# Reordering the start of a two-layer transformer kernel: the DMA queue's order and the first tile's place on TensorE

## The chip, the core and the metric

The kernel runs on one core of a Trainium2 chip. The core has a matrix engine (TensorE, PE in the profile), a vector engine (VectorE, DVE), an activation engine (ScalarE, ACT), a general engine (GpSimd, POOL) and a sync engine (SyncE, SP) that here only issues DMAs. Each engine works through its own instructions in order and waits on semaphores where it needs another's result. SP, ACT and POOL can issue DMAs, and the profile counts 16 DMA engines that carry them.

The metric is the device time of one execution in microseconds (us). The kernel before was timed three times: 1159.06, 1164.08 and 1165.76 us, so its median is 1164.08 us. The execution that the profiler recorded took 1164.43 us.

## The reference, cut to what matters

Two layers work on `x` of shape (2, 1024, 256). Each layer normalises `x` and adds an attention and a feed-forward result to it. The change is in layer 0's attention, at its very beginning:

```python
xn = _layernorm(x)
q = (xn @ Wq + bq).reshape(B, T, 32, 8).transpose(0, 2, 1, 3)     # 32 heads of 8
k = (xn @ Wk + bk).reshape(B, T, 8, 8).transpose(0, 2, 1, 3)      # 8 K/V heads
v = (xn @ Wv + bv).reshape(B, T, 8, 8).transpose(0, 2, 1, 3)
q = q * cos + rotate_half(q) * sin
k = k * cos + rotate_half(k) * sin
scores = einsum('bhqd,bhkd->bhqk', q, repeat(k, 4)) / sqrt(8)
scores = where(kpos > qpos, -inf, scores)
out = einsum('bhqk,bhkd->bhqd', softmax(scores), repeat(v, 4)) @ Wo + bo
x = x + out + ffn(xn)                                             # then layer 1, of the same kind
```

## The kernel before

**Tiles and chunks.** The 2048 rows of `x` are 16 tiles of 128 (`xs[0]` to `xs[15]`) and 4 chunks of 512. Layer 0's attention (`attention0`) goes over query tiles `(b, i)`: batch 0 from `i = 0` to 7, then batch 1 from 7 down to 0. Tile `(0, 0)` is called the first tile here, `(0, 1)` the second, and so on. A chunk's Q and K are made by `project` (L829 the matmuls, L840 the multiplication with the rope table on DVE), written to DRAM in three bf16 parts and read back in another layout.

**Two passes over a tile.** A softmax needs each row's maximum. So each tile has a pass of `max_unit`s (L992 the products, L964 the mask, L1004 the reduction on DVE), one for each pair of heads or for a few of them; then `take_max` (L1012) splits the 32 maxima of each row into three parts, `turn_max` (L1025) turns them on PE, copies them on ACT (`mts`, L1029), writes them to DRAM (`mscr`, L1031) and reads them back as three more rows of the Q tile (`qlast<-mscr`, L1033). With these rows the second product subtracts the maximum by itself. This second pass is `weigh` (L1056): the tile's scores `s`, their exponential `p` on ACT (L1066), the causal triangle on POOL (L1070), and `gather` (L1086), which adds up `p` times V in PSUM.

**The order on PE is written out.** In `attention0` the order of PE's instructions is the order in which Python emits them. `one_slot` (L1281) is the clock: each slot lets `advance` emit some `max_unit`s, in an order and at a rate worked out beforehand, with one step from `extra` (layer norm, projections of chunk 1, and so on) after a unit; then `tick` runs what `after(slots, f)` had put off. The main loop (L1301) does `weigh` for a tile, one pair of heads and K block per slot, but first runs slots without `weigh` until the tile's `take_max` lies `LEAD` slots back, or `SHORT` slots for the first three tiles. `wait_busy` (L1269) puts matmuls without use in front of a unit: 55 in front of unit 0, and 10 in front of unit 5, the first one of the second tile.

**The DMA queue.** Nearly all transfers of this stretch are issued by SP, in one order. In the first chunk, `prepare_q` (L881) sends the first tile's part of Q to DRAM from ACT and keeps the three other tiles' parts, two writes each, in `unsent`. `load_q` (L906) then reads a tile back with eight transfers: per half, two of 24 rows by 4 KB, one of 16 rows and one of 8 rows. The loop at L1156 emits for tiles 1, 2 and 3 the two writes and then the eight loads, with chunk 1 of `x` (four tiles) after tile 1. Then follow `bo`, the rope table of chunk 1 (`load_rope(1)`), `wo` and the eight tiles of `x` of batch 1. `issue_after(ins)` only orders an instruction behind `ins` on its engine. SP's transfers share eight semaphores in turn, and one whose semaphore is still in use by the eighth transfer before it waits for that one.

Of the kernel before, what the change touches and what calls it, by code (L numbers as in the profile page):

```python
# [37 lines left out]
TAIL = 16  # L38
LEAD = 10
SHORT = 6  # L40
LN_EPS = 1e-5
RMS_EPS = 2.0**-23
E4_MIN = 2.0**-6
# [5 lines left out]
def two_layers(ctx: ExitStack, tc: tile.TileContext, a: dict, out: bass.AP):  # L49
# [9 lines left out]
    def load_x(lo, hi):  # L59
        for i in range(lo, hi):  # L60
            nc.sync.dma_start(out=xs[i], in_=x_flat[i * P : (i + 1) * P, :])
# [43 lines left out]
    def load_rope(c):  # L105
        nc.sync.dma_start(out=rope[:, :, c * 512 : (c + 1) * 512], in_=a["rope0"][:, :, c * 512 : (c + 1) * 512])
# [7 lines left out]
    def load_weights(pool, names):  # L114
        w = []
        for name in names:
            n = a[name].shape[1]
            t = pool.tile([P, 2, n], F32, tag=name, name=name)
            nc.sync.dma_start(out=t, in_=a[name].rearrange("(k p) n -> p k n", p=P))
            w.append(t)  # L120
        return w
# [17 lines left out]
    def keep_busy(out, n):  # L139


        rhs = ident_bf[:, None, :].to_broadcast([P, 4, P])
        for _ in range(n):
            nc.tensor.matmul(out.rearrange("p (h q) -> p h q", h=4), groups, rhs, start=True, stop=True)  # L144
# [14 lines left out]
    def behind():  # L159
        return tc.issue_after(mark[0].ins)  # L160

    def rsqrt(pool, src, n, eps, name):

        v = pool.tile([P, n], F32, tag="rs_v", name=f"rs_v{name}", bufs=1)
        s = pool.tile([P, n], F32, tag="rs_s", name=f"rs_s{name}", bufs=1)
        y = pool.tile([P, n], F32, tag="rs_y", name=f"rs_y{name}", bufs=2)
        nc.vector.tensor_scalar(v, src, eps, None, ALU.add)
        nc.scalar.activation(s, v, AF.Sqrt)
        nc.vector.reciprocal(y, s)
        nc.vector.tensor_mul(s, y, y)  # L170
        nc.vector.tensor_mul(s, s, v)
        nc.vector.tensor_scalar(s, s, -0.5, 1.5, ALU.mult, ALU.add)
        nc.vector.tensor_mul(y, y, s)
        return y

    def layernorm(L, chunks, lp, pp, tag):
# [4 lines left out]
        for i in range(n):  # L181
# [3 lines left out]
            if i % 4 == 3:  # L185
                yield
        rs = rsqrt(lp, mv[:, :n, 1], n, LN_EPS, f"ln{nm}")
        yield
# [583 lines left out]
    def attention0(w, qlast, tables):  # L772
# [11 lines left out]
        with ExitStack() as es:  # L784
# [8 lines left out]
            last_load = [None]  # L793
# [112 lines left out]
            def load_q(b, i):  # L906

                qst[b, i] = [
                    pool.tile([P, NH0 // 2, P], BF, tag="qmain", name=f"qmain_{b}{i}", bufs=len(qlast)),
                    qlast[len(qst) % len(qlast)],  # L910
                ]
                for e in range(2):
                    parts = scratch[b, i, e].rearrange("a (d h) t -> a d (h t)", d=HD0)
                    for n, row, lo, hi in ((0, 0, 0, 3), (0, 24, 0, 3), (0, 48, 0, 2), (1, 0, 2, 3)):
                        row += HALF * e
                        last_load[0] = nc.sync.dma_start(
                            out=qst[b, i][n][row : row + HD0 * (hi - lo)].rearrange("p h t -> p (h t)"),
                            in_=parts[lo:hi],
                        )
# [5 lines left out]
            def prepare_v(b, c):  # L925
                v = vst[b]
                for kt in range(4 * c, 4 * c + 4):
                    ps = ps_t.tile([P, KV0, HD0], F32, tag="t", name=f"vp0_{b}_{kt}")
                    for k in range(2):
                        nc.tensor.matmul(  # L930
                            ps.rearrange("p g d -> p (g d)"),
                            xnT[2 * b + kt // 4][:, k, (kt % 4) * P : (kt % 4 + 1) * P],
                            wv[:, k, :],
                            start=(k == 0),
                            stop=(k == 1),
                        )
                    nc.vector.tensor_tensor(
                        v[:, kt, :, 0:HD0], ps, bv_bc.rearrange("p (g d) -> p g d", d=HD0), ALU.add
                    )


            slot = 0
            later = []

            def after(slots, f):
                later.append((slot + slots, f))
# [25 lines left out]
            def wait_busy(n):  # L972
                if n:
                    keep_busy(ps_t.tile([P, 512], F32, tag="t", name=f"busy{slot}_{n}"), n)
# [37 lines left out]
            def take_max(b, i):  # L1012
                both = mx.pop((b, i))
                m = both[:, 0].rearrange("p e n -> p (e n)")
                parts = pool.tile([P, 3, NH0], BF, tag="mparts", name=f"mp{b}{i}", bufs=1)
                r = pool.tile([P, NH0], F32, tag="mrest", name=f"mr{b}{i}")
                if i > 3:
                    nc.vector.tensor_tensor(both[:, 0], both[:, 0], both[:, 1], ALU.min)
                nc.vector.tensor_copy(parts[:, 0], m)
                nc.vector.tensor_tensor(r, m, parts[:, 0], ALU.subtract)  # L1020
                nc.vector.tensor_copy(parts[:, 1], r)
                nc.vector.tensor_tensor(parts[:, 2], r, parts[:, 1], ALU.subtract)
                after(3, lambda: turn_max(b, i, parts))

            def turn_max(b, i, parts):  # L1025
                ps = ps_t.tile([P, P], BF, tag="t", name=f"mt{b}{i}")
                nc.tensor.transpose(ps[: 3 * NH0], parts.rearrange("p a h -> p (a h)"), ident_bf)
                mt = pool.tile([3 * NH0, P], BF, tag="mt", name=f"mts{b}{i}", bufs=2)
                nc.scalar.copy(mt, ps[: 3 * NH0])  # L1029
                scr = dram.tile([3 * NH0, P], BF, tag="mscr", name=f"mscr{b}{i}")  # L1030
                nc.sync.dma_start(out=scr, in_=mt)  # L1031
                for e in range(2):
                    nc.sync.dma_start(  # L1033
                        out=qst[b, i][1][HALF * e + AUG : HALF * e + AUG + 3],
                        in_=scr.rearrange("(a e n) t -> e a n t", a=3, e=2)[e],
                    )
# [116 lines left out]
                prepare_q(0, 0, e)  # L1153
            load_q(0, 0)

            for i in range(1, 4):  # L1156
                with tc.issue_after(last_load[0].ins):
                    for j, send in unsent:
                        if j == i:
                            last_load[0] = send(nc.sync, i)  # L1160
                with tc.issue_after(last_load[0].ins):
                    load_q(0, i)
                if i == 1:
                    with tc.issue_after(last_load[0].ins):
                        load_x(4, 8)
            with tc.issue_after(last_load[0].ins):
                nc.sync.dma_start(out=bo_bc, in_=a["bo"][None, :].to_broadcast([P, D]))
            with behind():
                prepare_v(0, 0)
                for _ in range(3):  # L1170
                    next(conversions)
            with tc.issue_after(last_load[0].ins):
                load_rope(1)
                (wo,) = load_weights(zp, ("wo0",))
            with tc.issue_after(last_load[0].ins):
                load_x(8, NT)
# [80 lines left out]
            at = 0  # L1257
# [4 lines left out]
            done_at = {}  # L1262

            def advance():
                nonlocal at, credit, cost_left
                n, cost, unit = maxima[at]
                ready.extend(extra.pop(n, ()))

                wait_busy({0: 55, 4 + 1: 10}.get(at, 0))  # L1269
                unit()  # L1270
                if ready:
                    ready.pop(0)()
                at += 1
                credit -= cost
                cost_left -= cost
                if cost == 0:
                    done_at[n] = slot
                    if n >= 3:
                        next_weights()
# [21 lines left out]
            for n, (b, i) in enumerate(order):  # L1301
                if n and n + 3 < len(order):
                    load_q(*order[n + 3])
                while n not in done_at or slot < done_at[n] + (LEAD if n > 2 else SHORT):
                    one_slot(False)
                for G in range(2):
                    for j in range(i + 1):
                        for u in range(2):
                            one_slot(True)
                            if u and waiting:  # L1310
                                gather(*waiting)
                            group += weigh(b, i, 2 * G + u, j)
                        waiting = (b, i, G, j, group)
                        group = []
# [109 lines left out]
```

## Time and profile before

| What | us |
|---|---|
| three runs | 1159.06, 1164.08, 1165.76 |
| the profiled execution | 1164.43 |
| its span, first to last instruction | 1162.7 |
| PE busy | 1007.4 (87%) |
| DVE busy | 788.7 (68%) |
| ACT busy | 589.0 (51%) |
| POOL busy | 407.1 (35%) |
| first max unit of the first tile on PE | 42.64 |
| first product of the second tile on PE | 56.90 |
| first `weigh` of the first tile | 92.95 |

The span is what the trace covers; the device time of the same execution is 1.7 us more. A busy share is an average over both layers. What the change is worth is read from the first 140 us, where layer 0's attention starts. In the timeline each row gives the start, the duration, the engine, the line, the operation with what it writes and reads, how many of them are merged in the row, and in brackets how long the engine was idle before it and what ended that. `SPq` rows are DMA issues: they show when SP issued a transfer, not when it landed. Landings come from the trace's semaphore events.

### The profile page before, as it was taken

The page shows a single profiled execution, that of the slowest core. Times are in us where ns is not written, and L with a number is a line of the kernel's source. Part 1 is how long each engine was busy: PE and PEld are TensorE (multiplying, and loading weights), DVE is VectorE, ACT ScalarE, POOL GpSimd, SP SyncE. Part 2 cuts the span into 40 slices and gives each one's busy share as a digit, 9 for nine tenths or more (in the row PEclk, how much of TensorE's full clock was granted, in tenths as well). Part 3 has the DMA queues.
Part 4 walks back from the last instruction along what each step waited for, and adds up shares of the span by engine and source line. Part 5 has one row for each costly group of instructions (what it writes and reads, how often), then busy time and mean ns, then how long its engine had stood idle before and what let it go on. Part 6 is the DMA issues. An engine that isn't in the chain of part 4 may idle for free. (4 is left out here: it accounts for less than half of the span.)

```text
span 1162.7 us, 19973 instructions
## 1 busy us (share of the span) xinstructions
PE 1007.4 (87%) x7671; PEld 483.5 (42%) x7707; DVE 788.7 (68%) x1476; ACT 589.0 (51%) x1061; POOL 407.1 (35%) x440
## 2 busy tenths in 40 slices
PE   5858786887988989897989999885999999999798
PEld 3333331232432312232223333323567667667576
DVE  7467988899697998789896988605453554444421
ACT  2004461674456757576876777754354443443431
POOL 2007223424136121412134244547444535433400
PEclk9758896998899989998999999998899999989889
DMA  5432101101102010100000100007611432341200
GB/s 177 118 109 70 48 2 39 21 21 42 53 2 55 1 28 10 29 18 7 22 8 21 27 13 19 5 1 92 92 38 39 74 77 51 59 88 34 39 20 20
DMA packets 65928, 49.05 MB, mean 42 GB/s; under 512 B 20904, under 2 KB 59432, under 8 KB 65832
## 3 DMA queue, kind: packets, MB, share of 16 engines
q1 hardware_dynamic: 60632, 39.05, 15.0%
q0 software_dynamic: 4112, 8.26, 3.0%
q8 instruction: 60, 0.98, 0.4%
q10 hardware_dynamic: 1088, 0.46, 0.1%
q14 instruction: 36, 0.29, 0.1%
HBM read 34.12 MB, written 15.20 MB: 42 GB/s over the span
## 5 line engine op out<-in xcount | busy, mean ns | idle before, releaser
L1004 DVE TENSOR_REDUCE mx<-m 128x1 f32<-128x512 f32 (+3 forms) x608 | 372.4, 653 | 91.9 <-PE m L992 53.7
L1066 ACT ACTIVATE p<-s 128x512 f32<-128x512 f32 x576 | 307.1, 606 | 132.1 <-PE s L1056 129.6
L1086 PE MATMUL acc<-p,v 128*9 128x512 f32 x1152 | 170.8, 612 | 2.4 <-ACT p L1066 1.2
L1070 POOL TENSOR_SCALAR_AFFINE_SELECT p<-p 128x512 f32<-128x512 f32 x128 | 84.3, 681 | 157.7 <-ACT p L1066 157.4
L992 PE MATMUL m<-k,qmain 64*128 64x512 bf16 (+3 forms) x384 | 94.3, 356 | 49.7 <-DVE mx L1004 39.2
L992 PE MATMUL m<-kmain,qmain 64*128 64x512 bf16 (+3 forms) x384 | 83.1, 333 | 24.8 <-DVE mx L1004 22.7
L992 PEld LDWEIGHTS <-qmain 64*128 64x128 bf16 x768 | 50.1, 99 | 79.8 <-issue 50.9
L964 PEld LDWEIGHTS <-ident_h 64*128 64x128 bf16 x832 | 45.4, 97 | 88.0 <-issue 65.1
L964 PE MATMUL m<-mask_q,ident_h 64*128 64x128 bf16 (+3 forms) x832 | 75.0, 221 | 2.4 <-DVE mx L1004 2.2
L1056 PE MATMUL s<-qmain,k 64*128 64x512 bf16 x288 | 67.9, 395 | 9.0 <-ACT ob L275 3.1
L673 POOL TENSOR_TENSOR sq<-h 128x512 f32<-128x512 f32 x28 | 29.1, 1039 | 118.1 <-DVE h L669 118.1
L1056 PE MATMUL s<-qmain,kmain 64*128 64x512 bf16 x288 | 64.3, 390 | 5.3 <-ACT p L1066 2.6
L1056 PE MATMUL s<-qlast,k 35*128 35x512 bf16 x288 | 63.9, 390 | 0.0
L514 DVE TENSOR_REDUCE m<-sq 128x16 f32<-128x2048 f32 x16 | 36.7, 2291 | 37.9 <-PE sq L506 36.3
L1056 PEld LDWEIGHTS <-k 64*128 64x128 bf16 (+1 forms) x576 | 21.1, 95 | 97.7 <-issue 89.6
L1056 PE MATMUL s<-qlast,klast 35*128 35x512 bf16 x288 | 61.3, 387 | 0.0
L659 PEld LDWEIGHTS <-wgu_bf 128*128 128x128 bf16 x384 | 38.4, 101 | 42.0 <-issue 5.8
L1129 POOL TENSOR_TENSOR x<-x,aos 128x256 f32<-128x256 f32 x16 | 12.0, 747 | 116.0 <-ACT aos L1128 116.0
L668 DVE SCALAR_TENSOR_TENSOR h<-h,f1gu 128x512 f32<-128x512 f32 x32 | 22.0, 686 | 41.7 <-ACT h L667 41.7
L697 PE MATMUL f1o<-k,hp 128*128 128x256 bf16 x384 | 46.1, 279 | 1.0 <-ACT vts L532 0.7
L541 PE MATMUL sk<-qs,ks 25*128 25x128 f32 x512 | 43.8, 423 | 3.1 <-DMA qs<-mscr 3.1
L457 PE MATMUL pqk<-k,xnT 128*128 128x512 f32 x64 | 37.5, 717 | 9.7 <-ACT all L478 9.3
(289 smaller groups left out, 1800.3 us busy)
## 6 DMA issues: line engine op xcount, KB each, us to landing
qmain<-qscr SPq DMA_DIRECT2D x64, 96.0 KB
qkv<-all SPq DMA_DIRECT2D x16, 384.0 KB
qscr<-ptq POOLq DMA_DIRECT2D x6, 384.0 KB, 4.2
x<-in_x SPq DMA_DIRECT2D x16, 128.0 KB
qmain<-qscr SPq DMA_DIRECT2D x32, 64.0 KB
qs<-qkv SPq DMA_DIRECT2D x16, 128.0 KB
ks<-qkv SPq DMA_DIRECT2D x16, 128.0 KB
vs<-qkv SPq DMA_DIRECT2D x16, 128.0 KB
```

Source lines behind the costliest of these rows:

```text
L457: nc.tensor.matmul(pqk, x[k], wqk[:, k, :], start=(k == 0), stop=(k == 1))
L514: nc.vector.tensor_reduce(m, ps, AX.X, ALU.max, negate=True)
L541: nc.tensor.matmul(ps[:, s, r, :], columns(k, slice(S * s, S * s + HD + 9), 4 * b + r), columns(q, slice(S * s, S * s + HD + 9), 4 * b + r ...
L659: nc.tensor.matmul(ps[g], wgu_bf[:, k, g * HID + hc * P : g * HID + (hc + 1) * P], x_parts[n][m][:, k, :], start=(k == 0 and m == 0), stop ...
L697: nc.tensor.matmul(po, hs[hc][:, m, i * P : (i + 1) * P], wp[:, hc, :], start=(hc == 0 and m == 0), stop=(hc == NHC - 1 and m == 2),)
L964: nc.tensor.matmul(out[e][:, :, lo:], ident_h[rows, t, :], rhs.to_broadcast([HALF, out[e].shape[1], P - lo]), start=start and t == 0, stop ...
L992: nc.tensor.matmul(sc[e][:, s * width : (s + 1) * width], qst[b, i][0][rows, p, :], kst[b][0][rows, lo // 512, p // 4, 0:width], start=not ...
L1004: reduced = nc.vector.tensor_reduce(mx[b, i][:, part, e, pairs[0] : pairs[0] + n], sc[e][:, : n * width].rearrange("p (s k) -> p s k", s=n ...
L1056: nc.tensor.matmul(sc[e], kst[b][n][rows, j // 4, u, j % 4 * P : (j % 4 + 1) * P], qst[b, i][n][rows, 4 * u : 4 * u + 4, :], start=n == 0, ...
L1066: nc.scalar.activation(p, sc[e], AF.Exp, scale=scale)
L1070: nc.gpsimd.affine_select(out=by_head, in_=by_head, compare_op=ALU.is_ge, fill=0.0, base=0, pattern=[[0, 4], [1, P]], channel_multiplier=-1,)
L1086: nc.tensor.matmul(acc[32 * s : 32 * s + HD0 + 1, :], vst[b][:, j, 4 * G + s, :], ps[s], start=(j == 0), stop=(j == i),)
```

## The change

Four edits, all at the beginning of layer 0's attention:

1. The six writes of the tiles 1 to 3 (two each) are emitted together, ahead of the loads of tile 1.
2. After the loads of tile 1 come chunk 1 of `x` and, newly here, chunk 1 of the rope table; then the loads of the tiles 2 and 3, then `bo`. `load_rope(1)` no longer stands behind `bo`.
3. For the first tile, `turn_max` is put off by 1 slot instead of 3, and `weigh` may begin 4 slots (`FIRST`) after `take_max` instead of 6 (`SHORT`).
4. Five useless matmuls in front of unit 4 (the first tile's `take_max`, which has no PE work of its own) take the place of ten in front of unit 5.

```diff
+FIRST = 4
@@ take_max
-                after(3, lambda: turn_max(b, i, parts))
+
+                after(3 if b or i else 1, lambda: turn_max(b, i, parts))
@@ attention0
-            for i in range(1, 4):
+
+            def in_queue(f):
                 with tc.issue_after(last_load[0].ins):
+                    f()
+
+            def send_others():
+                for i in range(1, 4):
                     for j, send in unsent:
                         if j == i:
                             last_load[0] = send(nc.sync, i)
-                with tc.issue_after(last_load[0].ins):
-                    load_q(0, i)
-                if i == 1:
-                    with tc.issue_after(last_load[0].ins):
-                        load_x(4, 8)
-            with tc.issue_after(last_load[0].ins):
+
+            def load_bo():
                 nc.sync.dma_start(out=bo_bc, in_=a["bo"][None, :].to_broadcast([P, D]))
+
+            in_queue(send_others)
+            in_queue(lambda: load_q(0, 1))
+            in_queue(lambda: load_x(4, 8))
+            in_queue(lambda: load_rope(1))
+            for i in range(2, 4):
+                in_queue(lambda: load_q(0, i))
+            in_queue(load_bo)
...
             with tc.issue_after(last_load[0].ins):
-                load_rope(1)
                 (wo,) = load_weights(zp, ("wo0",))
@@ advance
-                wait_busy({0: 55, 4 + 1: 10}.get(at, 0))
+                wait_busy({0: 55, 4: 5}.get(at, 0))
@@ the main loop
-                while n not in done_at or slot < done_at[n] + (LEAD if n > 2 else SHORT):
+                while n not in done_at or slot < done_at[n] + (LEAD if n > 2 else SHORT if n else FIRST):
                     one_slot(False)
```

In the built program the orders on the engines change as follows. On PE the first tile's `turn_max` moves from behind the second tile's unit of pairs 6 and 7 to behind that of pairs 0 and 1. The first tile's `weigh` moves ahead: its first pair of heads now comes behind the second tile's pairs 12 and 13 and ahead of pairs 14 and 15, ahead of both Q projections of chunk 1 (`q010p`, `q011p`); before, it came behind both. The `weigh` of the second tile begins behind the third tile's pair 11 instead of pair 9. From the fourth tile's pair 7 on, PE has the same order in both programs, but for one swap of neighbours far behind. On SP, the write of the first tile's maxima (`mscr`) stood between the writes and the loads of tile 3, and its two reads (`qlast<-mscr`) behind the eight tiles of `x`; now the write, too, stands behind the eight tiles of `x`, directly ahead of its reads. The second tile's `mscr` moves from ahead of the loads of tile 4 to behind them, and its two reads stand behind the first two loads of chunk 1's K.

## The prediction

> **What bounds the kernel now.** I read the page's forty slices first, to see whether one engine bounds the whole. A slice is 29 us.
>
> ```profile
> PE   5858786887988989897989999885999999999798
> DVE  7467988899697998789896988605453554444421
> PEclk9758896998899989998999999998899999989889
> ```
>
> PE bounds most of the span, but its slices 1, 3 and 5 are half to eight tenths full: the start waits for data. The changed order meets the old one again at the fourth tile's pair 7 on PE, at 138 us in the trace. So the change is worth the lag or lead with which PE (and DVE, which reads the maxima) arrives there. Next the DMA queue's timeline (start, duration, issuing queue, line, output and input) says why PE waits.
>
> ```profile
> 53.80 2.01 SPq L896 DMA_DIRECT2D qscr<-ptq  x2
> 59.85 2.08 SPq L916 DMA_DIRECT2D qmain<-qscr  x3
> ...
> 66.44 1.61 SPq L1031 DMA_DIRECT2D mscr<-mts  x1
> 71.04 2.11 SPq L916 DMA_DIRECT2D qmain<-qscr  x3
> ...
> 77.05 0.63 SPq L106 DMA_DIRECT2D rope<-in_rope  x1
> 78.52 0.40 SPq L119 DMA_DIRECT2D wo<-in_wo  x1
> 78.97 7.98 SPq L61 DMA_DIRECT2D x<-in_x  x8
> 87.00 0.62 SPq L1033 DMA_DIRECT2D qlast<-mscr  x2
> ```
>
> A tile's loads go out only when its writes have landed, so the queue runs empty ahead of tiles 2 and 3. The rope table is issued at 77.05, and the first tile's maxima come back last. Then the timeline of PE and DVE shows who waits for what (in brackets the idle time before a row, and what ended it).
>
> ```profile
> 76.19 6.01 PE L829 MATMUL q010p<-xnT,wq 128*128 128x512 f32 x8
> 86.07 1.41 DVE L840 SCALAR_TENSOR_TENSOR q010y<-q010p,bq,rope 128x512 f32<-128x512 f32 x2 [8.29 <-DMA rope<-in_rope]
> 86.87 0.47 PE L992 MATMUL m<-k,qmain 64*128 64x384 bf16 x1 [4.40 <-DVE q010y L840]
> 87.53 5.48 PE L829 MATMUL q011p<-xnT,wq 128*128 128x512 f32 x8
> 92.95 0.39 PE L1056 MATMUL s<-qmain,k 64*128 64x512 bf16 x2
> 93.93 3.70 PE L829 MATMUL k01p<-xnT,wk 128*128 128x512 f32 x8
> ```
>
> The rope table holds DVE for 8.29 us and PE behind it for 4.40. The maxima (landed at 89.87) hold nobody: PE gets to the first tile's `s` only at 92.95.
>
> **Edits 1 and 2: the queue.** First how fast it drains, since everything follows from it. In the trace's landings a load of 24 rows by 4 KB uses only three DMA engines, one of 16 rows two; the lowest-numbered engine carries 50 rows, 200 KB, of a tile's eight loads. Tile 2's eight land from 63.9 to 70.7 after an issue at 59.85, about 1.3 us for each eight rows: 7.9 us per tile in a running queue. Tile 3's land at 84.5, from 75.9 on: 9.8 us with the setup of the stretch, wide loads beside them. The Trainium skill has this rule ("DMA: Bandwidth & Descriptors", the section on why a semaphore counts by 16): a transfer uses the largest number of engines up to 16 that divides both row counts, beginning with the lowest. Its specifications give 27 GiB/s per engine and 435 GB/s for all. By the latter a tile's 576 KB would take 1.3 us and the queue would be empty before 68; by one engine's rate 200 KB takes 6.9 us (an estimate from that page). The trace says 7.9, so the narrow reading decides and I use 7.9 and 9.8.
>
> The four writes that move ahead take 0.27 us each on that engine (first landing 44.05, last 44.31), but most of it lies in the gap in which tile 1's loads start anyway (issued 44.11, first rows 45.2): +0.2. So tile 1 is there at 57.2 instead of 57.0. Both holes on the writes go, about 5 us of queue. Then in the new order: four tiles of `x` 2.6 (57.0 to 59.5 in the trace), rope 1.3 (84.66 to 85.96), so rope lands at **61.1** instead of 86.0; tile 2 69.0; tile 3 78.8 instead of 84.5; `bo` 0.2, `wo` 0.65, the eight `x` 2.9 (86.61 to 89.50): 82.5.
>
> The rope wait goes: 8.29 on DVE, 4.40 on PE. What is late next there is not the projection but what the third edit puts ahead of it.
>
> **The first tile's maxima.** Their write was issued at 66.44 between the queue's other work; now it stands behind the eight `x`, and SP waits in order, however early `mts` is ready. It lands at 82.6, its reads issue at 82.7 and 83.0, and they took 2.0 us when nothing was ahead (issued 105.64 and 105.92, landed 107.69 and 107.86). So the rows are there at **85.0**, 4.9 us earlier than before. Bounds: 83 if tile 3 too drains in 7.9, 88.5 if `x` is issued only as its semaphores come free one by one, as in the row of 7.98 us.
>
> **Edits 3 and 4: PE's order.** These put the first tile's `s` ahead of `q010p`, `q011p`, `k01p` and the second tile's pairs 14 and 15. When does PE arrive? The second tile's units run at DVE's pace: in the trace they end at 73.5 with 11.04 of 12 us busy on DVE.
>
> ```profile
> 60.00:72.00 12.00, 6.93 (x65) 5.03 (x66) 11.04 (x29) 1.54 (x4) 0.00 (x0) 0.50 0.23 69
> ```
>
> (The columns are window, length, PE, weight loads, DVE, ACT, POOL, clock, DMA share, GB/s.) Nothing in the edits makes DVE's part shorter; the removal of ten matmuls without use at the second tile and five more at 4 is hidden, as the first hides in the wait for tile 1's loads (3.03 us). So PE stands at `s` from 73.5 to 85.0: a new wait of **11.5 us**, with pairs 14 and 15, the third tile's units, both Q projections, K's and V's behind it in line; behind those wait DVE's `q010y`, the casts on ACT and the selects on POOL. Before, PE used 76.19 to 82.20 of this for `q010p`.
>
> From 85.0: the last two products of `s` and pair 14 take 1.2, the turnover of the three buffers that `q010p` shares with the maxima 1.4 (an estimate, two reductions of 0.7 each), `q010p` 4.8: the first four at the half clock 3.0 (half of 6.01), the rest at full 1.8 (half of 3.70). The second multiplication of `q010y` starts at 92.4, against 86.8 before: **+5.6**. From there to the reduction of the third tile's pair 4 (103.13 in the trace) were 16.3 us. `q011p` is now wholly warm, 3.7 for 5.48: -1.8; the first tile's further `s`, its gathers and selects, which stood elsewhere, +1.5. So pair 4 is at 108.4, **+5.3**.
>
> On the clock, the Trainium skill ("TensorE: Matmul & The Clock Gate", part 1, what is actually happening) speaks against this change: one idle window of some 3.4 us halves the clock, and as much sustained work restores it. In the trace `q010p` at 0.50 takes 6.01 and `k01p` at full 3.70, and full clock came 4.5 us after PE resumed at 86.87. By the rule the restart costs 3.4 x 0.5 = 1.7, by the trace 2.2; PE is at half clock here before the change too, so neither adds to the sum; I use the trace's delay in splitting `q010p`.
>
> **The second tile's maxima.** They used to be written ahead of tile 4's loads (issued 101.73, read 105.64). Now they are behind them, and their reads also behind the first two loads of K. `kscr` was issued 21.3 us after `q010y`, so about 113.7 now; landing 5 to 6.5 later, then K's two loads and these rows 5.6 (2 x 1.8 for 16 rows, 2.0 for the rows): about 125. PE is there at 118.7. This second wait of about 6 costs DVE, which has its own maxima queued, about 3 to 4.5.
>
> ```profile
> 120.00:140.00 20.00, 12.91 (x100) 5.57 (x95) 19.93 (x55) 8.04 (x16) 5.58 (x8) 0.89 0.15 53
> ```
>
> DVE is full from 120 to 140 (19.93 of 20), so nothing there absorbs a lag. Against it: with the first tile's `weigh` ahead, PE has 3.3 us of such work less to do after pair 4. The sum: +5.3, +3.5 to 4.5 for the second wait, -1 to -2 for the work done ahead: **+8**, so 1164.4 + 8 = **1172 us**. The profiled 1164.43 stands beside the median 1164.08, so nothing is corrected.
>
> **Rivals.**
> - *The lag is mostly work done ahead.* The same two waits, but the second is short (kscr lands early, PE arrives late), and the 3.3 us of `weigh` and the 1.8 of warm clock count fully: 5.3 - 3.3 + 1 = +3, **1167**. For it: 90 to 110 has spare time on DVE (14.1 busy of 20). Against it: 120 to 140 has none.
> - *Faster: the queue drains first.* The first maxima's rows land before PE comes. It is one mechanism: loads queued without holes use the idle DMA engines (share 0.23 to 0.29 at 57 to 80), or the write of the maxima overtakes on engines that the loads leave free. The deciding point is T = 76.6: each us of landing after it is a us lost. At T = 73.5 no wait is left, the rope wait of 8.3 is gone, and what remains is PE's and DVE's work: about -8, **1156**. For it: only three of 16 engines are busy. Against it: the reads wait for SP, which must first issue all that is ahead, and engine 0 is the slow one.
> - *Slower still.* `x` trickles (88.5), the second wait counts in full on DVE: 5.3 + 3.5 + 6.5 = +15, **1180**.
> - *It doesn't do it.* The built program shows the order as told, so I give this nothing of its own.
>
> **How the numbers follow.** Forecast 0.55, work ahead 0.24, faster 0.15, slower still 0.06. The forecast's own range is 1168 to 1178 (T from 83 to 88.5, the second wait from 2 to 6). The range for 8 in 10 takes in the second case whole and leaves most of the third and fourth: **1159 to 1179**. A measurement of this kernel tells about 0.5%, 5.8 us, from no change: 1158.3 to 1169.9. Faster: the third case, with a little from the second, **0.17**. Same: most of the second and the low end of the forecast, **0.28**. Slower: **0.55**.
>
> **What would show each step.** In the changed profile: the rope table issued by 56, tile 2's loads right behind without a hole, and no wait of `q010y` on rope. Right or wrong on the decisive step: the first tile's `s<-qlast` on PE, idle before it some 11 us, ended by `qlast<-mscr` at about 85; if PE goes through it by 77, the forecast is wrong in sign. Then the second multiplication of `q010y` at 92, the third tile's pair 4 at 108 on DVE, and a second wait on `qlast<-mscr` between 119 and 125. If both waits stand as told but the fourth tile's pair 7 comes before 138, the work done ahead was worth more than I gave it.

## The result and the profile after

| | us | against before |
|---|---|---|
| before, four runs | 1163.91 median (1159.06 to 1165.76) | |
| the changed kernel, four runs | 1177.97 median (1176.34 to 1179.43) | ratio 1.0122, 95% interval 1.0093 to 1.0151 |
| the changed kernel's profiled execution | 1177.07, span 1175.3 | span 12.6 more |

The change makes the kernel slower by 14 us, or 1.2%. The forecast was 1172 in a range of 1159 to 1179: the right side, the right cause, and some 6 us too little, near the upper end of the range.

The page's forty slices of the changed kernel come first (tenths of a slice; the prediction shows the same lines of before):

```profile
PE   5748686889888989898889999896899999989898
DVE  7457789899787997879897888705354454444431
PEclk9758687999799989999899999999899899989889
```

On PE the third slice falls from 5 to 4 and the fifth from 7 to 6, where the granted clock falls from 8 to 6. Those are the stretches of 59 to 88 and of 118 to 147 us. Here is SP's timeline of the changed kernel:

```profile
54.37 0.63 SPq L107 DMA_DIRECT2D rope<-in_rope  x1
56.19 3.25 SPq L917 DMA_DIRECT2D qmain<-qscr  x3
...
74.29 6.65 SPq L62 DMA_DIRECT2D x<-in_x  x8
81.06 0.36 SPq L1033 DMA_DIRECT2D mscr<-mts  x1
82.97 0.57 SPq L1035 DMA_DIRECT2D qlast<-mscr  x2
...
115.04 0.32 SPq L1033 DMA_DIRECT2D mscr<-mts  x1
119.80 1.45 SPq L875 DMA_DIRECT2D k<-kscr  x2
121.34 0.70 SPq L1035 DMA_DIRECT2D qlast<-mscr  x2
```

The rope table goes out 23 us earlier than before (77.05), and tile 2's loads follow it without the hole. But both `mscr` rows are late. PE turned the first tile's maxima at 59.05, and ACT copied them right behind:

```profile
59.42 0.26 ACT L1031 COPY mts<-mt 96x128 bf16<-96x128 bf16 x1 [23.41 <-PE mt L1029]
```

So they are ready at 59.7, and SP issues their write only at 81.06. The second tile's write stands at 115.04 behind tile 4's loads: the main loop emits these when it comes to the second tile, and with the first tile's `weigh` moved ahead that is now before the second tile's `turn_max`. PE's timeline at the rows that read the maxima:

```profile
73.31 0.38 PE L1058 MATMUL s<-qmain,k 64*128 64x512 bf16 x1
84.91 0.76 PE L1058 MATMUL s<-qlast,k 35*128 35x512 bf16 x2 [11.22 <-DMA qlast<-mscr]
...
87.75 4.70 PE L830 MATMUL q010p<-xnT,wq 128*128 128x512 f32 x8
...
125.64 0.76 PE L1058 MATMUL s<-qlast,k 35*128 35x512 bf16 x2 [6.91 <-DMA qlast<-mscr]
```

In the bracket stands how long PE was idle and what ended it: two waits, 11.22 and 6.91, both for the maxima's rows. `q010p` starts at 87.75, where before it started at 76.19. DVE's timeline carries this on:

```profile
92.48 0.75 DVE L841 SCALAR_TENSOR_TENSOR q010y<-q010p,bq,rope 128x512 f32<-128x512 f32 x1 [0.63 <-PE q010p L830]
...
108.26 3.07 DVE L1005 TENSOR_REDUCE mx<-m 128x1 f32<-128x384 f32 x6
...
126.87 1.02 DVE L1005 TENSOR_REDUCE mx<-m 128x1 f32<-128x384 f32 x2 [6.22 <-PE m L965]
130.18 2.06 DVE L1005 TENSOR_REDUCE mx<-m 128x1 f32<-128x384 f32 x4 [2.29 <-PE m L965]
```

The wait for rope is gone from `q010y`; it waits 0.63 for PE instead. At 108.26 begins the third tile's pair 4 (103.13 before). And the second wait of PE leaves DVE idle for 6.22 and 2.29. Compare the windows from 110 to 140 of the two kernels (length, then busy time of PE, weight loads, DVE, ACT, POOL, then clock, DMA share and GB/s), before:

```profile
110.00:140.00 30.00, 21.43 (x169) 8.94 (x169) 29.91 (x73) 11.95 (x23) 10.08 (x13) 0.93 0.19 65
```

and after:

```profile
110.00:140.00 30.00, 18.31 (x125) 7.17 (x124) 21.19 (x47) 6.66 (x12) 9.29 (x8) 0.62 0.15 48
```

DVE was full (29.91 of 30) and now stands for 8.8 us. A full engine has no idle time in this stretch with which to make that up.

Matching the same DVE instructions of the two traces gives the lag along the way. It is 1.0 at 44 us, ahead of anything that the change touches (starts differ like that from run to run), 12.6 where before stood at 128, 13.6 at 148, 12.8 at 290, 12.6 at 310 and 12.3 at 1158. Nothing behind the first 150 us gives or takes more than some 1 us for long. So the whole difference arises in the stretch that the prediction worked out.

### The profile page after: what moved, and what is told of

Read it like the earlier page. It is cut to its first block, busy times and chain, and to the rows that moved or that the text cites. A ratio compares the mean times of both kernels' runs of the same rounds, so it can differ in the third digit from the quotient of the medians.

```text
span 1175.3 us, 19949 instructions
## 1 busy us (share of the span) xinstructions
PE 1006.3 (86%) x7666; PEld 481.7 (41%) x7702; DVE 788.5 (67%) x1476; ACT 589.2 (50%) x1061; POOL 407.9 (35%) x440
## 5 line engine op out<-in xcount | busy, mean ns | idle before, releaser
L1058 PE MATMUL s<-qlast,k 35*128 35x512 bf16 x288 | 66.0, 400 | 18.1 <-DMA qlast<-mscr 18.1
```

The source lines that it names most:

```text
L1058: nc.tensor.matmul(sc[e], kst[b][n][rows, j // 4, u, j % 4 * P : (j % 4 + 1) * P], qst[b, i][n][rows, 4 * u : 4 * u + 4, :], start=n == 0, ...
```

## The experiments

The theory to be tested: edit 3 moves the first tile's `s` to a place that PE reaches before the rows can be there, and all of the loss lies in the two waits on `qlast<-mscr`. The first rival is that the queue's new order (edits 1 and 2) costs by itself; the second is that the new order on PE costs by itself, by the clock or by the selects on POOL. Each ratio below is against the kernel before, timed beside the run, with its 95% interval.

### The queue's edits alone

Edits 1 and 2 stay, edits 3 and 4 are undone.

```diff
-                after(3 if b or i else 1, lambda: turn_max(b, i, parts))
+                after(3, lambda: turn_max(b, i, parts))
-                wait_busy({0: 55, 4: 5}.get(at, 0))
+                wait_busy({0: 55, 4 + 1: 10}.get(at, 0))
-                while n not in done_at or slot < done_at[n] + (LEAD if n > 2 else SHORT if n else FIRST):
+                while n not in done_at or slot < done_at[n] + (LEAD if n > 2 else SHORT):
```

> Edits 1 and 2 alone (the queue's order), the first tile's turn, its 6 slots and the ten useless matmuls as before. The second tile's maxima are written ahead of tile 4's loads here, as before the change. My theory (the loss is PE waiting twice on qlast<-mscr): rope lands near 61, q010y doesn't wait for it, PE reaches the first tile's s near 88.5 when the rows (landed near 85) are there; no wait on qlast<-mscr of over 1 us; 4 us less than before, about 1160 (1157 to 1163). Rival (the queue's new order is itself what costs: writes ahead of loads, maxima behind eight x): slower than before by 5 or more, 1169 and above.

Measured: 1166.11, ratio 1.0003 (0.9982 to 1.0025). So the queue's order doesn't carry the loss, and the rival falls. But the gain of 4 that the theory named isn't there either. DVE led by 5.5 at the first multiplication of `q010y`, by 4.0 at 90 us, and at 109 it lagged by 2.0. Where the lead went is shown by ACT's timeline of this run:

```profile
91.77 0.62 ACT L805 CAST ptq<-q011y 128x512 bf16<-128x512 f32 x1 [4.16 <-POOL q011y L845]
93.65 0.62 ACT L809 CAST ptq<-restq 128x512 bf16<-128x512 f32 x1 [1.26 <-POOL restq L806]
94.29 1.28 ACT L1068 ACT_TABLE_LOAD   x1
95.58 1.09 ACT L1068 ACTIVATE p<-s 128x512 f32<-128x512 f32 x2
```

compared with ACT's timeline before,

```profile
93.59 0.60 ACT L1066 ACTIVATE p<-s 128x512 f32<-128x512 f32 x1 [0.65 <-PE s L1056]
95.55 0.62 ACT L804 CAST ptq<-q011y 128x512 bf16<-128x512 f32 x1 [1.36 <-POOL q011y L844]
```

and by PE's timeline of this run:

```profile
105.11 3.27 PE L1088 MATMUL acc<-p,v 128*9 128x512 f32 x4 [2.05 <-POOL p L1072]
```

The first tile's `s` was complete at 87.8, but its exponential `p` stands in ACT's order behind all four casts of Q, which wait for POOL; it runs at 95.58. Before, the first `p` ran at 93.59, between the casts. The selects and `acc`, which need it, come so late that the whole lead is used up: behind the removed wait stood one on ACT and POOL. This is taken up again below.

### The order's edits alone

Edits 3 and 4 on the queue of before: the first diff's lines the other way round.

> Edits 3 and 4 alone (the first tile's turn after 1 slot, its weigh after 4, five useless matmuls), the queue as before. My theory: PE stands at the first tile's s from about 74 until the second half of the maxima's rows comes behind the eight x, near 89.9: a first wait of 15 to 16 us, and a second one near 120 of 6 to 7, since the second tile's maxima again stand behind tile 4's loads; about 18 more than before, 1182 (1176 to 1187). Rival (the queue is what costs): within 0.5% of before.

Measured: 1181.74, ratio 1.0131 (1.0074 to 1.0188). PE's timeline:

```profile
90.99 0.58 PE L1057 MATMUL s<-qlast,k 35*128 35x512 bf16 x1 [16.48 <-DMA qlast<-mscr]
129.07 0.76 PE L1057 MATMUL s<-qlast,k 35*128 35x512 bf16 x2 [3.65 <-DMA qlast<-mscr]
```

The first wait is 16.48, just above the 15 to 16 that was expected; the second is about half of what was expected. Edits 3 and 4 together cost 1.3% without the queue's edits and 1.2% with them. Edit 4 shows no effect of its own (below), so edit 3 is the part that makes the kernel slower.

### The second tile's maxima ahead of tile 4's loads

```diff
                 if n and n + 3 < len(order):
-                    load_q(*order[n + 3])
+                    if n > 1 or order[1] in turned:
+                        load_q(*order[n + 3])
+                    else:
+                        behind_turn[order[1]] = lambda: in_queue(lambda: load_q(*order[4]))
```

`turn_max` calls what `behind_turn` holds for its tile as soon as it has emitted the reads of the maxima, and the loads are ordered behind these.

> The whole change, but tile 4's loads are emitted behind the second tile's maxima, so that their write and reads stand ahead of these loads and of K's. My theory: the first wait stays (11 us, to 85), the second of 6.9 goes, and with it the 8.5 us that DVE stood there: 1178 - 8.5 = 1169.5 (1167 to 1172). Rival (the first wait alone makes the lag, the second only shows it, as DVE or the loads of tile 4 would be late anyway): 1175 or more.

Measured: 1169.53, ratio 1.0040 (1.0024 to 1.0057), so 9.5 us less than the whole change (1.0122 - 1.0040, times 1164; by the two intervals, give or take 4). The waits of PE in its profile, in the stretch from 60 to 130 (total, times, longest), have one line left on these rows:

```profile
PE s L1062 <- DMA qlast<-mscr: 11.0, 1, 11.0
```

The second wait is gone, and with it a part of the time, so it isn't a mere sign of the first. But not all of the 8.5 us that DVE stood there belongs to it. Here are DVE's waits for the maxima's products from 108 to 155 (total, times, longest), in the changed kernel and in this run:

```profile
DVE mx L1005 <- PE m L965: 9.3, 4, 6.2
DVE mx L1005 <- PE m L965: 2.2, 3, 1.5
```

The difference is 7.1, about the 6.91 of PE's wait. The other 2.2 stay without any wait for rows, most of them (1.5) where PE does `acc` before DVE's next maxima; the kernel before has no such wait of DVE in this stretch. They belong to the new order on PE.

### Both tiles' maxima ahead

In addition, tile 3's loads, `bo`, `wo` and the eight `x` are emitted behind the first tile's maxima.

```diff
-            for i in range(2, 4):
-                in_queue(lambda: load_q(0, i))
-            in_queue(load_bo)
+            in_queue(lambda: load_q(0, 2))
+            def rest_of_queue():
+                in_queue(lambda: load_q(0, 3))
+                in_queue(load_bo)
...
+            behind_turn = {(0, 0): rest_of_queue}
```

> As before this one, and tile 3's loads, bo, wo and the eight x are emitted behind the first tile's maxima too, so that these are written and read directly behind tile 2's loads. My theory: the rows are there at 71 to 73, PE comes at 73.5 and doesn't wait; q010p follows at the half clock. The lag of 5 at the third tile's pair 4 turns to a lead of about 4: 1178 - 8.5 - 9.5 = 1160 (1156 to 1164). Rival (the order on PE costs by itself, by the clock or the selects on POOL): both waits are gone and it is still slower than before, 1168 or more.

Measured: 1161.93, ratio 0.9973 (0.9956 to 0.9990). SP's timeline:

```profile
62.94 0.31 SPq L1036 DMA_DIRECT2D mscr<-mts  x1
69.75 0.55 SPq L1038 DMA_DIRECT2D qlast<-mscr  x2
...
97.60 0.33 SPq L1034 DMA_DIRECT2D mscr<-mts  x1
99.89 0.57 SPq L1038 DMA_DIRECT2D qlast<-mscr  x2
```

The first rows are read from 69.75 on, and no wait for a maximum is left on PE. The same order on PE, with only the queue changed, is now faster than before, so the order on PE by itself isn't what makes the change slower, and the second rival falls as well. What this order is worth against the old one is measured at the end of this part.

### The first tile's maxima ahead, the second's not

The last diff without the one ahead of it.

> The whole change, but tile 3's loads, bo, wo and the eight x are emitted behind the first tile's maxima; the second tile's maxima stay behind tile 4's loads. If the two waits add up, this gains what the run with both gained over the run with the second alone, 1169.5 - 1161.9 = 7.6: about 1170 (1167 to 1173), with a second wait of about 7 on PE, since K's projection and what waits for it move ahead together. Rival (the waits are one delay passed on: with the first gone the second goes or shrinks): 1165 or less. Second rival (the second grows by what the first gave up): 1176 or more.

Measured: 1166.35, ratio 1.0009 (0.9990 to 1.0027), just below the range that was expected. PE's timeline:

```profile
112.46 0.78 PE L1065 MATMUL s<-qlast,k 35*128 35x512 bf16 x2 [4.43 <-DMA qlast<-mscr]
```

The second wait is still there, 4.43 here, not 7. Against the whole change this run gains 13 us (0.0113 x 1164), the one with the second tile's alone 9.5, and both together 17.3. The two single gains exceed this by some 5, but by the intervals that is uncertain by 5 as well. In the traces they add up: DVE's lag where before stood at 148, less its lag at 44, is 12.5 in the changed kernel, 7.3 with the second tile's maxima ahead, -0.8 here and -5.6 with both. That makes gains of 5.2, 13.3 and 18.1. So the second wait isn't the first one's delay passed on.

### Only the eight x behind the maxima

```diff
-            with tc.issue_after(last_load[0].ins):
-                load_x(8, NT)
+            behind_turn = {(0, 0): lambda: in_queue(lambda: load_x(8, NT))}
```

> The whole change, but only the eight x are emitted behind the first tile's maxima; tile 3's loads, bo and wo stay ahead of them. By the sum on record the eight x take 2.9 us of queue, and each us in which the rows land later than PE comes is a us lost: rows at 82 instead of 84.9, first wait 8.3 instead of 11.2, the time 3 less than with the whole change, 1175 (1173 to 1176.5). Rival (the wait on the first maxima is cover for something else up to the end): no difference, 1178.

Measured: 1173.08, ratio 1.0085 (1.0053 to 1.0116). PE's timeline:

```profile
81.73 1.04 PE L1062 MATMUL s<-qlast,k 35*128 35x512 bf16 x2 [7.52 <-DMA qlast<-mscr]
119.78 0.76 PE L1062 MATMUL s<-qlast,k 35*128 35x512 bf16 x2 [3.33 <-DMA qlast<-mscr]
```

The first wait is 3.7 shorter and the second 3.6 shorter; the time falls by about 4 (0.0037 x 1164), with intervals that overlap. By its median it lies in what was expected of the time, but the second wait wasn't expected to move. Why it did is taken up under what stays open.

### The rope table alone

The kernel before, with one transfer moved.

```diff
                     with tc.issue_after(last_load[0].ins):
                         load_x(4, 8)
+                    with tc.issue_after(last_load[0].ins):
+                        load_rope(1)
...
-                load_rope(1)
```

> Before the change, with the rope table of chunk 1 moved behind the four x, nothing else: DVE's wait of 8.3 on rope is gone, and the first tile's maxima come back near 90 as before. In the run with the queue's edits alone a lead of 7.8 at q010y was gone by 112, behind the casts on ACT and the selects on POOL. If that chain takes any lead, this is within 0.5% of before, 1165 (1161 to 1169). Rival (it was the maxima behind the eight x that took it in that run, and a lead from rope is kept): 1160 or less. The wait on qlast<-mscr may come out at 1 to 3 us here, as PE arrives near 88.

Measured: 1166.73, ratio 1.0019 (1.0000 to 1.0039): no gain. The wait of 8.29 is gone and DVE leads by 6.5 at the first multiplication of `q010y` (in the run with the queue's edits alone it was 5.5, not the 7.8 of the text on record); at 111 the lead is gone. Part of it goes to the rows that were hidden behind the rope table, in PE's timeline:

```profile
89.48 0.76 PE L1056 MATMUL s<-qlast,k 35*128 35x512 bf16 x2 [3.34 <-DMA qlast<-mscr]
```

The rest goes as in the first experiment: the order on ACT is the same as there, with the first `p` behind all casts of Q.

### Edit 4 undone

`wait_busy` as in the first diff, all else as in the change.

> The whole change without edit 4: ten useless matmuls in front of unit 5 again, none in front of unit 4. They lie in the wait for the second tile's loads and in DVE's pace, so nothing changes by over 2 us: 1178 (1176 to 1180). Rival (the clock in this stretch carries part of the loss): 3 or more less, 1175 or below.

Measured: 1177.66, ratio 1.0111 (1.0079 to 1.0143): no difference from the whole change that this measurement shows. In its profile the first wait is 10.50 and the second 3.81, where the changed kernel's profile has 11.22 and 6.91.

### Both tiles' maxima ahead, PE's order as before

What the first experiment left open: does ACT's order take the lead, or would POOL and DVE take it whatever ACT does? With the rows early, the program is built with ACT's `p` between the casts again.

> The queue as in the run with both maxima ahead (first tile's behind tile 2's loads, second tile's ahead of tile 4's), but edits 3 and 4 undone: PE's order at the start is that of before. Against the run with the queue's edits alone, the built order on ACT differs: the first tile's first exponentials stand between the casts of Q, as before the change, instead of behind all four of them. Theory: that place behind the casts is what ate the lead of 5.8 in that run; here 4 or so is kept: 1161.5 (1159 to 1163). Rival (POOL's and DVE's work on chunk 1's Q and K bounds this stretch whatever ACT's order): 1165 or more. If the theory holds and it equals the run with both ahead, edit 3 is worth nothing even with the rows on time.

Measured: 1163.51, ratio 0.9986 (0.9964 to 1.0008). By the time alone it decides nothing. The profile says more. ACT's timeline:

```profile
87.75 0.62 ACT L809 CAST ptq<-restq 128x512 bf16<-128x512 f32 x1 [1.48 <-POOL restq L806]
88.39 1.28 ACT L1075 ACT_TABLE_LOAD   x1
89.68 0.60 ACT L1075 ACTIVATE p<-s 128x512 f32<-128x512 f32 x1
92.53 0.62 ACT L805 CAST ptq<-q011y 128x512 bf16<-128x512 f32 x1 [2.25 <-POOL q011y L845]
```

The first `p` runs at 89.68 instead of 95.58, and DVE still leads by 3.0 at 107, where the first experiment had lost all: there it lagged by 2.2 at the same instruction. But right behind, in PE's timeline,

```profile
110.10 0.58 PE L1065 MATMUL s<-qlast,k 35*128 35x512 bf16 x1 [1.82 <-DMA qlast<-mscr]
```

both of the second tile's reads (issued at 105.41 and 105.86) had slipped behind the first two of tile 4's loads (103.83 and 104.63), and the lead was gone. So the next run holds these reads in place:

```diff
-                    if n > 1 or order[1] in turned:
+                    if n > 1:
                         load_q(*order[n + 3])
+                    elif order[1] in turned:
+                        with tc.issue_after(turned[order[1]].ins):
+                            load_q(*order[4])
...
+                        with tc.issue_after(turned[0, 1].ins):
                             stacks(scr)
```

> As the run with early rows and edits 3 and 4 undone, and the second tile's reads held wholly ahead of tile 4's loads and of K's; in the last run one of them came behind the first of these loads, PE waited 1.8 and 0.4 us for them at 110, and a lead of 3.0 was gone behind it. Theory (ACT's order keeps the lead, that wait took it): PE doesn't wait at 110 and the lead lasts, 3 to 4 less than before, about 1161 (1159 to 1163). Rival (DVE's pace behind 110 takes any lead): 1163.5 as the last run, or more.

> The kernel with both tiles' maxima ahead again, beside the one without edits 3 and 4 on the same chip, for what edit 3 is worth when the rows are on time. If edit 3 is worth nothing then: within 2 us of that run. If it is worth PE's work put ahead: 3 or more less than it. By the earlier comparison with before: 0.3% less than before, 1161 to 1163.

Measured on the same chip: 1160.75, ratio 0.9957 (0.9942 to 0.9973), for the first, and 1162.05, ratio 0.9971 (0.9956 to 0.9985), for the second. No wait for the maxima is left in the first, and its lead at 111 (2.2) is kept: 2.0 at 185. So with `p` between the casts the lead lasts, and the short wait for the second tile's rows had taken it. ACT's order, and with it the place of POOL's selects, was not changed by itself: the queue differs as well between the first experiment and these. But in none of them did PE wait for the first tile's rows. And edit 3 is worth nothing even when the rows are on time: without it the kernel is the faster of the two by 0.14%, less than the intervals can tell.

## Why the prediction was right, and where it was too small

Its steps against the trace:

| Step | predicted | in the trace |
|---|---|---|
| rope issued | by 56 | 54.37 |
| PE arrives at the first `s` | 73.5 | 73.3 |
| the first tile's rows are there | 85.0 | 84.9 |
| first wait | 11.5 | 11.22 |
| `q010p` | 4.8 | 4.70 |
| second multiplication of `q010y` | 92.4 | 92.48 |
| third tile's pair 4 | 108.4 | 108.26 |
| the second tile's rows are there | about 125 | 125.6 |
| second wait on PE | about 6 | 6.91 |
| **what DVE stands at it** | **3 to 4.5** | **8.5** |
| work done ahead (fall of the lag from 148 to 310) | -1 to -2 | -1.0 |

**The queue.** The narrow reading (a tile's loads drain at the pace of the engine with most rows) gave 85.0, and the rows were there at 84.9. (Its "row counts" are the outermost counts of both sides: the source of a load of 24 rows is three parts of 8 rows, so the counts are 3 and 24, and three engines come out.) It also decided against the faster rival: PE comes 11 us too early for rows that stand behind two tiles' loads, `bo`, `wo` and eight `x`. The experiments with the maxima ahead show that this rival named the right mechanism and more than twice its price: with the rows read from 69.75 on both waits vanish, and what is left is some 3 us faster than before (ratios 0.9973 and 0.9971), not 8.

**The term that was too small** is the second wait's. The prediction put it as "costs DVE, which has its own maxima queued, about 3 to 4.5". It measured 8.5: 6.22 at the wait, and 2.29 where PE then does `acc` before DVE's next maxima. Two things were wrong in it. First, the queued maxima cover hardly any of the wait, 0.7 of 6.91, since PE, which makes them, is the engine that stands. Seven profiles with edit 3's order, among them five with a second wait, show what it costs DVE:

| Run | second wait of PE | DVE's waits for PE, 108 to 155 |
|---|---|---|
| the changed kernel | 6.91 | 9.3 |
| the first tile's maxima ahead | 4.43 | 7.0 |
| edit 4 undone | 3.81 | 6.3 |
| the order's edits alone | 3.65 | 6.2 |
| only the eight `x` behind | 3.33 | 5.8 |
| the second tile's maxima ahead | none | 2.2 |
| both tiles' maxima ahead | none | 2.9 |

Above the 2 to 3 us of the last two rows, each us of the wait is about a us of DVE. Second, some 2 to 3 us stand there with no second wait at all. The prediction put what the new order on PE does to DVE in this stretch at nothing.

With 8.5 in that place the prediction's sum reads 5.3 + 8.5 - 1 to 2, some 12. The spans differ by 12.6 (1.0 of it from the start, ahead of the change) and the medians by 14. The size is that of one profiled execution: with only edit 4 undone, an execution of 1174.76 us had a second wait of 3.81. The "slower still" rival had this half right (the second wait in full on DVE) and its other half wrong (the `x` did not hold the rows until 88.5).

**Edits 1 and 2** were credited with 8.29 on DVE and 4.40 on PE, as a wait that goes and is followed by edit 3's. Alone they bring nothing (1.0003), and the rope table alone nothing (1.0019). In the sum on record the gain wasn't counted by itself, so this didn't disturb the total; but the expectation of 4 for the queue alone left out what was late next.

**The rival in which the lag is mostly work done ahead** falls: the lag at 148 us (13.6) was still 12.3 at the end.

**Edit 4** made no difference that shows, as the sum had it. The clock was not tested by itself. One hit on it was part luck: `q010p` took 4.70 where the sum had 4.8. The prediction read the 6.01 of before as eight products at the half clock, but the granted clock there rose from 0.50 to full at 80.91. At 3.70 for eight at full clock, one at the half clock takes about 0.92 (an estimate), not 0.75. In the changed kernel the clock rose at 89.79, so that about two of the eight ran at the half clock, not four.

**What stays open.** Why the second wait came out at 6.91 in the changed kernel and at 3.33 in the run with only the eight `x` behind, with the same order on PE, is explained in part. The rows come behind K's write. In the changed kernel PE stood at the second tile's `s` 4.9 us after POOL issued this write, in the other run 7.0 us after. These 2.1 us are mostly the turn that POOL and DVE took just ahead (below): it made POOL's `ptk` 1.0 longer in the one, and DVE, at whose pace PE comes, 0.9 slower in the other. The other 1.5 us are the landing of the write, 6.0 us after its issue in the one and 4.5 in the other. Why the landing differed wasn't tried.

## What to carry to other kernels

Before work is moved ahead on one engine, follow its last operand through every queue that carries it, in the order as built: here the maxima were ready at 60, but their write stood behind 20 us of loads, so that the "earlier" work became an 11 us wait at the head of an engine that works in order. A wait on the engine that feeds a full one is not covered by what is queued between them: here each us of PE's second wait was a us of DVE, and the lag was still there a thousand us later. And a removed wait (8.3 us for the rope table) brought nothing until the next two in line, here `p` behind the casts on ACT and the second tile's rows, were out of the way too: then edits 1 and 2, with the rows early, gave 0.4%.

## What the runs showed of the hardware

POOL and DVE took turns at one pair of two-operand elementwise instructions on float32 tiles. In the changed kernel DVE's `fsw` began first; the rows of DVE and POOL:

```profile
111.25 1.22 DVE L219 TENSOR_TENSOR fsw<-spare_last,few 128x1024 f32<-128x1024 f32 x1
111.35 2.13 POOL L810 TENSOR_TENSOR ptk<-restk,ptk 128x512 bf16<-128x512 f32 x1 [0.73 <-ACT ptk L809]
```

In the run with only the eight `x` behind, POOL's began first:

```profile
107.95 1.15 POOL L810 TENSOR_TENSOR ptk<-restk,ptk 128x512 bf16<-128x512 f32 x1 [0.73 <-ACT ptk L809]
108.06 2.13 DVE L219 TENSOR_TENSOR fsw<-spare_last,few 128x1024 f32<-128x1024 f32 x1
```

Whichever begins 0.1 us later takes 2.13 instead of 1.15 or 1.22, that is, about its own time behind the other's. The two instructions overlap in twelve of the thirteen profiles, and in all twelve the later one is the long one (1.99 to 2.15). In the thirteenth, the rope table alone, they don't overlap, and they take 1.16 and 1.22. A microsecond of a chain on POOL can so be decided by who comes first. It doesn't hold for every pair: at 860 us of the kernel before, POOL's `hp` (1.16) and DVE's `h` (0.69), which has one operand in PSUM, ran side by side for 0.69 us, and neither took longer than usual. Why this pair takes turns wasn't tested.
